# Layer 0's norm and projection in a four-layer float32 kernel: 1/std applied token-major behind two projections

## The chip, the cores and the metric

The kernel runs on one core of a Trainium2 chip. The metric is the device time of one execution, in microseconds (us). A core has five engines with queues of their own: PE (matrix products; loads of its stationary operand are shown as PEld), DVE (vector), ACT (scalar functions), POOL and SP. In this kernel SP issues nearly all transfers.

## The reference

Four layers run one after the other on x of 2 x 64 x 64 x 128 float32, that is 2 batches of 4096 tokens with 128 channels. Only the end of layer 0 matters here. Layer 0 scans 256 inner channels in four directions, and the sum of the four is y. Then it takes a layer norm over the 256 channels, gates with silu(z), projects back to 128 channels and adds to x:

```python
m = mean(y, channels); v = var(y, channels)
n = (y - m) / sqrt(v + 1e-5) * ln_w + ln_b      # per token, 256 channels
x = x + (n * silu(z)) @ W_out.T                  # 256 -> 128 channels
```

(These lines are a short form of the norm, the gate and the projection.) After it come layer 1 (a deformable convolution, which needs all of x), layer 2 (a scan with 256 states and a long convolution) and layer 3.

## The kernel before, in words

`layer0` loops over the two batches b. Each goes through three stages, and the pools of one stage are closed before the next opens:

1. The input: transposes of x (`to_channels`, L95), group norm, the products for z and for the inner channels, a 3 x 3 convolution. silu(z) is written to a DRAM buffer `zs` (L211). Stage 1 ends with the inner channels in `U`.
2. The scans (L349 to L406), under an order written out by hand. The result adds up in `Y`, a tile of 128 partitions by 2 halves by 4096 tokens: channels lie on partitions, half h holds channels 128h to 128h+127.
3. The norm and projection (L408 to L436), which the change rewrites. Here the Tile framework's planner orders the instructions on every engine from the program's order and its own costs; no order is written by hand.

Stage 3 loops over 8 pieces q of N = 512 tokens. For each piece:

- SP loads `zt`, the silu(z) of the piece, 512 KB (L414).
- PE forms the mean `pm`: a product of `mean_w`, a 128 x 128 matrix of 1/256, with Y. Its 512 columns all hold the mean, repeated on all 128 partitions (L417).
- DVE subtracts it from both halves of Y (L420), ACT squares into `sq` (L421), PE forms the variance `pq` in the same way as the mean (L424).
- `rsqrt` (L81 to L87) works on 128 x 512 elements, since every partition holds its copy: add eps, ACT's Sqrt, DVE's reciprocal, then one Newton step of four DVE instructions.
- DVE multiplies by ln_w and 1/std (L429), adds ln_b and multiplies by zt (L430), each for two halves.
- PE projects: for each of four blocks j of 128 tokens the stationary operand is Y's block and the moving one `w_out`, so that tokens come out on partitions (`po`, L434). DVE adds po to `Xb` (L436), which is x with tokens on partitions.

The pool `wk` has 2 buffers per tile, the PSUM pool `ps` has 6 buffers that all of pm, pq and po share.

Of the kernel before, what the change touches and what calls it, by code (L numbers as in the profile page):

```python
# [16 lines left out]
F32 = mybir.dt.float32  # L17
I32 = mybir.dt.int32
BF16 = mybir.dt.bfloat16
AF = mybir.ActivationFunctionType  # L20
ALU = mybir.AluOpType
# [4 lines left out]
P = 128  # L26
B, HH, WW, C = 2, 64, 64, 128
# [3 lines left out]
N = 512  # L31
# [45 lines left out]
def rsqrt(nc, pool, out, var, eps, shape, tag):  # L77

    v = pool.tile(shape, F32, name=f"{tag}_v", tag=f"{tag}_v")
    s = pool.tile(shape, F32, name=f"{tag}_s", tag=f"{tag}_s")  # L80
    nc.vector.tensor_scalar(v, var, eps, None, ALU.add)  # L81
    nc.scalar.activation(s, v, AF.Sqrt)
    nc.vector.reciprocal(out, s)
    nc.vector.tensor_tensor(s, out, out, ALU.mult)
    nc.vector.tensor_tensor(s, s, v, ALU.mult)
    nc.vector.tensor_scalar(s, s, -0.5, 1.5, ALU.mult, ALU.add)
    nc.vector.tensor_tensor(out, out, s, ALU.mult)  # L87
# [71 lines left out]
def layer0(k):  # L159
    tc, nc, ins, X = k.tc, k.nc, k.ins, k.X  # L160
    T = N
    NC = L // T
    with ExitStack() as es:
        enter = es.enter_context
        cst = enter(tc.tile_pool(name="l0c", bufs=1))
# [11 lines left out]
            nc.vector.tensor_copy(sel[a : a + 16], k.ident[a : a + 16, a : a + 16].unsqueeze(2).to_broadcast([16, 16, P]))  # L177
        w_out = cst.tile([P, 2, C], F32, name="w_out")
        nc.sync.dma_start(out=w_out, in_=ins["w_out0"].rearrange("(a p) c -> p a c", p=P))
        mean_w = cst.tile([P, P], F32, name="mean_w")  # L180
        nc.vector.memset(mean_w, 1.0 / 256)
        an = cst.tile([P, 8, 16], F32, name="an")
# [9 lines left out]
        for b in range(B):  # L192
            Xb = X[:, b * NTB : (b + 1) * NTB, :]
            with ExitStack() as e2:
                pre = e2.enter_context(tc.tile_pool(name=f"l0p{b}", bufs=1))
                wk = e2.enter_context(tc.tile_pool(name=f"l0w{b}", bufs=3))
                ps = e2.enter_context(tc.tile_pool(name=f"l0ps{b}", bufs=6, space=PSUM))
# [41 lines left out]
            Y = yb.enter_context(tc.tile_pool(name=f"l0y{b}", bufs=1)).tile([P, 2, L], F32, name="Y")  # L239

            with ExitStack() as e2:
                ch = e2.enter_context(tc.tile_pool(name=f"l0h{b}", bufs=2))
                sm = e2.enter_context(tc.tile_pool(name=f"l0s{b}", bufs=1))
                wk = e2.enter_context(tc.tile_pool(name=f"l0k{b}", bufs=3))
                bcp = e2.enter_context(tc.tile_pool(name=f"l0e{b}", bufs=2, space=DRAM))
                ps = e2.enter_context(tc.tile_pool(name=f"l0ys{b}", bufs=1, space=PSUM))
# [102 lines left out]
                with tc.manual_schedule():  # L349
                    rows, pcn, last, save = spread(ready[0][1], 0), c_row(ready[0][2], 0), None, None  # L350
                    for it, (kk, ci) in enumerate(todo):
                        c = at(it)[1]
                        uc, bc, cs, dt, du, ea = ready.pop()
                        f = T - 1 if kk >= 2 else 0
# [51 lines left out]
                    add_up(*last)  # L406

            with ExitStack() as e2:  # L408
                wk = e2.enter_context(tc.tile_pool(name=f"l0f{b}", bufs=2))
                ps = e2.enter_context(tc.tile_pool(name=f"l0fs{b}", bufs=6, space=PSUM))  # L410
                for q in range(8):
                    s = slice(q * N, (q + 1) * N)
                    zt = wk.tile([P, 2, N], F32, name="zt")
                    nc.sync.dma_start(out=zt, in_=zs[:, :, b * L + q * N : b * L + (q + 1) * N].rearrange("h p t -> p h t"))  # L414
                    pm = ps.tile([P, N], F32, name="pm", tag="ps")
                    for h in range(2):
                        nc.tensor.matmul(pm, mean_w, Y[:, h, s], start=h == 0, stop=h == 1)  # L417
                    sq = wk.tile([P, 2, N], F32, name="sq")
                    for h in range(2):
                        nc.vector.tensor_tensor(Y[:, h, s], Y[:, h, s], pm, ALU.subtract)  # L420
                        nc.scalar.activation(sq[:, h, :], Y[:, h, s], AF.Square)  # L421
                    pq = ps.tile([P, N], F32, name="pq", tag="ps")
                    for h in range(2):
                        nc.tensor.matmul(pq, mean_w, sq[:, h, :], start=h == 0, stop=h == 1)  # L424
                    rs = wk.tile([P, N], F32, name="rs")
                    rsqrt(nc, wk, rs, pq, 1e-5, [P, N], "yn")
                    for h in range(2):
                        o = Y[:, h, s]
                        nc.vector.scalar_tensor_tensor(o, o, k.v("ln_w")[:, h : h + 1], rs, ALU.mult, ALU.mult)  # L429
                        nc.vector.scalar_tensor_tensor(o, o, k.v("ln_b")[:, h : h + 1], zt[:, h, :], ALU.add, ALU.mult)  # L430
                    po = ps.tile([P, N], F32, name="po", tag="ps")
                    for j in range(4):
                        for h in range(2):
                            nc.tensor.matmul(po[:, j * P : (j + 1) * P], Y[:, h, q * N + j * P : q * N + (j + 1) * P], w_out[:, h, :], start=h == 0, stop=h == 1)  # L434
                    o = Xb[:, 4 * q : 4 * q + 4, :]
                    nc.vector.tensor_tensor(o, po.rearrange("p (a c) -> p a c", c=C), o, ALU.add)  # L436
            yb.close()


# [944 lines left out]
def kernel(tc, ins, out, stages=STAGES):  # L1384
    nc = tc.nc
    with ExitStack() as es:
# [8 lines left out]
        if two or "0" in stages or "1" in stages:  # L1395
            with tc.tile_pool(name="x01", bufs=1) as xp:
                k.X = xp.tile([P, NT, C], F32, name="X")
                move(nc, k.X, tokens(x))
                if "1" in stages:
                    table = [dr.tile([TS * TS, 4 * C], F32, name=f"table{b}") for b in range(B)]  # L1400
                    with tc.tile_pool(name="zt", bufs=1) as zp:
                        zero_table(k, zp, table)
                mix = None
                if two:
                    weights, mix = mixing_weights(k, dr)
                if "0" in stages:
                    layer0(k)
                if "1" in stages:
                    layer1(k, table, mix)
                elif two:  # L1410
                    with ExitStack() as e2:
                        mix(e2)
                if two:
                    norm_tokens(k, rs, sh)
                x = dr.tile([B * L, C], F32, name="x1")
                move(nc, tokens(x), k.X)
# [119 lines left out]
```

## Time and profile before

| | us |
|---|---|
| median of 3 runs (15821.19 to 15835.69) | 15821.78 |
| the profiled execution | 15825.24 |
| its span in the profile | 15823.2 |
| stage 3, batch 0: first L417 to the end of L436 | 2102.7 to 2254.6 |
| stage 3, batch 1: first L417 to the end of L436 | 4341.7 to 4493.7 |

The durations come from the one profiled execution. A line of the timeline has the start, the duration, the engine, the line of the kernel, the operation, output <- input with their sizes, and how many instructions are merged; in brackets stands how long the engine sat idle before it and what it waited for. A line of busy time by stretch has, after the stretch and its length, the busy time and number of instructions of PE, PEld, DVE, ACT and POOL, then the granted clock of PE as a share of full speed, the share of DMA time and GB/s.

### The profile page before, as it was taken

Reading aid. Unit: us, or ns where it says so; the run is one execution under the profiler, and the core shown is the slowest. Engines: PE = TensorE matmul, PEld = TensorE weight load, DVE = VectorE, ACT = ScalarE, POOL = GpSimd, SP = SyncE. Lnnn points to the kernel's source line nnn. Section 1 sums busy time; section 2 is a strip of 40 time slices with the busy share of each in tenths; the row PEclk is TensorE's granted clock in tenths of the full one; section 3 lists DMA queues with packets and bytes.
Section 4 is the critical chain, followed back from the end, with each engine's and each line's share of the span. In section 5 each row is a group of like instructions: output and inputs, shape, how many; then the busy total and the mean of one; then the engine's idle time right before and its main releaser. Section 6 shows DMA issues by size and latency. Waiting matters only on the chain.

```text
span 15823.2 us, 190331 instructions
## 1 busy us (share of the span) xinstructions
PE 11939.5 (75%) x69390; PEld 7104.0 (45%) x69390; DVE 13880.2 (88%) x12178; ACT 9839.5 (62%) x15907; POOL 13460.9 (85%) x5140
## 2 busy tenths in 40 slices
PE   6666666666667744567887879879788898898897
PEld 2222222222247721234554546546445555555565
DVE  7999978999954389999999999999999999999974
ACT  5656626666510057777777777777777777777752
POOL 6888828888738889999999999999999999999960
PEclk9999989999978866778998989989999999999998
DMA  2111111111146534455565556556666665665643
GB/s 79 70 70 70 70 44 67 70 70 70 64 143 185 161 133 148 168 172 187 196 193 179 187 179 198 197 185 202 193 190 198 190 204 196 191 203 195 191 163 129
DMA packets 1211433, 2373.40 MB, mean 150 GB/s; under 512 B 346744, under 2 KB 923896, under 8 KB 1044352
## 3 DMA queue, kind: packets, MB, share of 16 engines
q1 hardware_dynamic: 1163072, 2206.74, 42.3%
q0 software_dynamic: 46560, 153.18, 3.2%
q8 instruction: 548, 8.98, 0.2%
q14 instruction: 389, 3.19, 0.1%
q10 hardware_dynamic: 864, 1.32, 0.0%
HBM read 2018.49 MB, written 342.41 MB: 149 GB/s over the span
## 4 chain that ended last, share of the span: by engine, by line
POOL 35%; PE 12%; DVE 11%; DMA 3%; ACT 2%; issue 2%; SPq 0%; POOLq 0%; ACTq 0%; DVEq 0%
POOL S L1110 34%; DVE S L1166 10%; PE pef L994 6%; PE Z L1128 2%; DMA row<-drow 2%; PE acc L967 2%; PE pw L793 1%; POOL S L1116 1%; ACT ze L1134 1%; ACT dA L1164 1%; DMA w<-in_w_b_dram 0%; PE acc L1029 0%; ACT e L974 0%; DMA e<-mdr 0%; PE pt L95 0%
## 5 line engine op out<-in xcount | busy, mean ns | idle before, releaser
L1166 DVE TENSOR_TENSOR_SCAN S<-dA,S 128x512 f32<-128x512 f32 x8192 | 9225.0, 1201 | 385.8 <-ACT dA L1164 207.0
L1110 POOL TENSOR_TENSOR S<-row,g 128x4096 f32<-128x4096 f32 x1024 | 9101.7, 8894 | 266.0 <-DMA row<-drow 224.2
L1164 ACT ACTIVATE dA<-row,a_t 128x512 f32<-128x512 f32 x8192 | 5615.6, 692 | 2141.3 <-DVE S L1166 2108.3
L1128 PE MATMUL Z<-S,cv 128*32 128x256 f32 x32768 | 2506.0, 436 | 1481.7 <-ACT ze L1134 1215.6
L994 PE MATMUL pef<-hk,ur 128*128 128x256 f32 x14336 | 3510.4, 388 | 131.8 <-ACT e L974 120.5
L994 PEld LDWEIGHTS pef<-hk,ur 128*128 128x128 f32 x14336 | 2645.3, 191 | 1070.8 <-issue 562.8
L376 DVE TENSOR_TENSOR_SCAN S<-dA,S 128x1024 f32<-128x1024 f32 x1024 | 2339.1, 2284 | 242.4 <-ACT dA L374 96.1
L365 POOL TENSOR_TENSOR S<-du,br 128x1024 f32<-128x1024 f32 x1024 | 2408.6, 2355 | 137.8 <-DVE M L390 81.0
L1128 PEld LDWEIGHTS Z<-S,cv 128*32 128x32 f32 x32768 | 1002.5, 121 | 2691.5 <-issue 1291.9
L405 PE MATMUL yp<-M,ident 128*128 128x512 f32 x4096 | 2054.6, 626 | 2.9 <-DVE M L390 2.9
L405 PEld LDWEIGHTS yp<-M,ident 128*128 128x128 f32 x4096 | 817.6, 200 | 2092.5 <-issue 2054.1
L374 ACT ACTIVATE dA<-dt,an 128x511 f32<-128x511 f32 x2048 | 1406.9, 687 | 208.1 <-DVE S L376 131.0
L390 DVE TENSOR_TENSOR M<-S,pcn 128x1024 f32<-128x1024 f32 x1024 | 1250.4, 1221 | 106.9 <-DVE S L376 3.7
L334 PE MATMUL pcn<-cs,sel 80*128 80x512 bf16 x1024 | 406.2, 397 | 1188.4 <-DVE M L390 1177.8
L1134 ACT COPY ze<-Z 128x512 f32<-128x512 f32 x1024 | 1123.1, 1097 | 232.4 <-PE Z L1128 200.3
L967 PE MATMUL acc<-e,mw 128*128 128x512 f32 x1920 | 1043.1, 631 | 30.6 <-ACT e L974 29.9
L569 POOL DMA_INDIRECT G<-table,idx x576 | 805.5, 1399 | 203.1 <-issue 170.6
L994 PEld LDWEIGHTS pef<-hd,ur 128*128 128x128 f32 x4096 | 757.8, 194 | 491.1 <-issue 235.2
L994 PE MATMUL pef<-hd,ur 128*128 128x256 f32 (+1 forms) x4096 | 876.4, 340 | 101.5 <-ACT e L974 94.4
L378 ACT COPY stt<-S 128x2 f32<-128x2 f32 x896 | 168.9, 189 | 1082.1 <-DVE S L376 1079.0
L576 DVE TENSOR_TENSOR G<-G,wt 128x4608 f32<-128x4608 f32 x64 | 317.4, 4960 | 572.9 <-DMA G<-table,idx 499.6
L974 ACT COPY e<-pef 128x512 f32<-128x512 f32 x960 | 557.8, 587 | 109.9 <-PE pef L994 61.5
(327 smaller groups left out, 8052.3 us busy)
## 6 DMA issues: line engine op xcount, KB each, us to landing
row<-drow SPq DMA_DIRECT2D x1024, 1024.0 KB
br<-bc SPq DMA_DIRECT2D x256, 1024.0 KB
zd<-ze SPq DMA_DIRECT2D x1024, 256.0 KB
hk<-in_phi_dram SPq DMA_DIRECT2D x128, 576.5 KB
hk<-in_phi_dram SPq DMA_DIRECT2D x96, 704.5 KB
hd<-in_phi_dram SPq DMA_DIRECT2D x512, 128.5 KB
mw<-wdr SPq DMA_DIRECT2D x480, 128.0 KB
hk<-in_phi_dram SPq DMA_DIRECT2D x160, 320.5 KB
```

The source lines that it names most:

```text
L365: nc.gpsimd.tensor_tensor(S, du, br[:, n % 4, :].unsqueeze(1).to_broadcast([P, 2, T]), ALU.mult)
L374: nc.scalar.activation(dA[:, h, rest], dt[:, h, rest], AF.Exp, scale=an[:, kk * 2 + h, n : n + 1])
L376: nc.vector.tensor_tensor_scan(flat, dflat, flat, 0.0, ALU.mult, ALU.add)
L390: nc.vector.tensor_tensor(M, S, pcn.unsqueeze(1).to_broadcast([P, 2, T]), ALU.mult)
L405: nc.tensor.matmul(yp[:, h, :], k.ident, M[:, h, :], start=False, stop=n == 15)
L967: nc.tensor.matmul(acc.rearrange("p a s -> p (a s)"), ms[f][:, o, :], e, start=box["first"], stop="whole" in box and (f, o) == todo[-1])
L994: nc.tensor.matmul(pe[:, a, 256 - n :], ur[:, par, j, :], h[:, at : at + n], start=i == 0, stop=i + 1 == len(mm))
L1110: nc.gpsimd.tensor_tensor(S, row.unsqueeze(1).to_broadcast([P, 2, R, T]), g.unsqueeze(2).to_broadcast([P, 2, R, T]), ALU.mult)
L1128: nc.tensor.matmul(Z[32 * j : 32 * j + 32, q], cv[:, h, s], S[:, h, :, s], start=h == 0, stop=h == 1)
L1134: nc.scalar.copy(ze.rearrange("p q t e -> p q e t"), Z)
L1164: nc.scalar.activation(dA, row[:, j % R, :], AF.Exp, scale=a_t[:, h, d : d + 1])
L1166: nc.vector.tensor_tensor_scan(s, dA, s, 0.0, ALU.mult, ALU.add)
```

## The change

- Two weight tiles are made once, on POOL, ahead of the batches: `w_ow` is w_out with each row times ln_w, `w_ob` is w_out with each row times ln_b.
- The norm's scale is taken out of the projection. With c = y - m, `po` is the projection of c * zt through `w_ow` and `pb` that of zt through `w_ob`. The sum is x + pb + po / std. Tokens lie on partitions there, so 1/std is one number per partition and block.
- The variance comes out token-major too: `pv` has one column per block j, from 8 products whose stationary operand is a block of sq and whose moving operand is one column of mean_w. `rsqrt` works on 128 x 4 elements.
- DVE multiplies Y by zt in one instruction of 128 x 1024; ACT squares in one of 128 x 1024.
- The body is cut in two functions, and `projected(q - 1)` is called behind `centred(q)`. The pool `wk` has 3 buffers.

```diff
+        w_ow = cst.tile([P, 2, C], F32, name="w_ow")
+        w_ob = cst.tile([P, 2, C], F32, name="w_ob")
+        for h in range(2):
+            nc.gpsimd.tensor_scalar(w_ow[:, h, :], w_out[:, h, :], k.v("ln_w")[:, h : h + 1], None, ALU.mult)
+            nc.gpsimd.tensor_scalar(w_ob[:, h, :], w_out[:, h, :], k.v("ln_b")[:, h : h + 1], None, ALU.mult)
...
-                wk = e2.enter_context(tc.tile_pool(name=f"l0f{b}", bufs=2))
+                wk = e2.enter_context(tc.tile_pool(name=f"l0f{b}", bufs=3))
                 ps = e2.enter_context(tc.tile_pool(name=f"l0fs{b}", bufs=6, space=PSUM))
-                for q in range(8):
+
+                def centred(q):
+
                     s = slice(q * N, (q + 1) * N)
...
                     for h in range(2):
                         nc.vector.tensor_tensor(Y[:, h, s], Y[:, h, s], pm, ALU.subtract)
-                        nc.scalar.activation(sq[:, h, :], Y[:, h, s], AF.Square)
-                    pq = ps.tile([P, N], F32, name="pq", tag="ps")
-                    for h in range(2):
-                        nc.tensor.matmul(pq, mean_w, sq[:, h, :], start=h == 0, stop=h == 1)
-                    rs = wk.tile([P, N], F32, name="rs")
-                    rsqrt(nc, wk, rs, pq, 1e-5, [P, N], "yn")
-                    for h in range(2):
-                        o = Y[:, h, s]
-                        nc.vector.scalar_tensor_tensor(o, o, k.v("ln_w")[:, h : h + 1], rs, ALU.mult, ALU.mult)
-                        nc.vector.scalar_tensor_tensor(o, o, k.v("ln_b")[:, h : h + 1], zt[:, h, :], ALU.add, ALU.mult)
-                    po = ps.tile([P, N], F32, name="po", tag="ps")
+                    nc.scalar.activation(sq, Y[:, :, s], AF.Square)
+                    nc.vector.tensor_tensor(Y[:, :, s], Y[:, :, s], zt, ALU.mult)
+                    return zt, sq
+
+                def projected(q, zt, sq):
+                    pv = ps.tile([P, N], F32, name="pv", tag="ps")
                     for j in range(4):
                         for h in range(2):
-                            nc.tensor.matmul(po[:, j * P : (j + 1) * P], Y[:, h, q * N + j * P : q * N + (j + 1) * P], w_out[:, h, :], start=h == 0, stop=h == 1)
+                            nc.tensor.matmul(pv[:, j : j + 1], sq[:, h, j * P : (j + 1) * P], mean_w[:, 0:1], start=h == 0, stop=h == 1)
+                    rs = wk.tile([P, 4], F32, name="rs")
+                    rsqrt(nc, wk, rs, pv[:, :4], 1e-5, [P, 4], "yn")
+                    po = ps.tile([P, 4, C], F32, name="po", tag="ps")
+                    pb = ps.tile([P, 4, C], F32, name="pb", tag="ps")
+                    for o, src, w in ((pb, lambda h, j: zt[:, h, j * P : (j + 1) * P], w_ob), (po, lambda h, j: Y[:, h, q * N + j * P : q * N + (j + 1) * P], w_ow)):
+                        for j in range(4):
+                            for h in range(2):
+                                nc.tensor.matmul(o[:, j, :], src(h, j), w[:, h, :], start=h == 0, stop=h == 1)
                     o = Xb[:, 4 * q : 4 * q + 4, :]
-                    nc.vector.tensor_tensor(o, po.rearrange("p (a c) -> p a c", c=C), o, ALU.add)
+                    nc.vector.tensor_tensor(o, pb, o, ALU.add)
+                    for j in range(4):
+                        nc.vector.scalar_tensor_tensor(o[:, j, :], po[:, j, :], rs[:, j : j + 1], o[:, j, :], ALU.mult, ALU.add)
+
+                behind = None
+                for q in range(8):
+                    got = centred(q)
+                    if behind is not None:
+                        projected(q - 1, *behind)
+                    behind = got
+                projected(7, *behind)
```

## The prediction

> **What bounds the kernel now.** I read the page's slices first, then the busy time by stretch, then the timeline of one piece. The slices of DVE dip where each batch of layer 0 ends (slice 5 covers 1978 to 2373 us), and TensorE's granted clock dips there too:
>
> ```profile
> DVE  7999978999954389999999999999999999999974
> ...
> PEclk9999989999978866778998989989999999999998
> ```
>
> The two stretches from the last addition into Y to the last addition into X, by busy time of each engine:
>
> ```profile
> core 0: us, PE busy (x) PEld busy (x) DVE busy (x) ACT busy (x) POOL busy (x), PEclk, DMA share, GB/s
> 2101.32:2254.59 153.27, 62.28 (x192) 36.89 (x192) 92.50 (x106) 16.06 (x25) 0.56 (x1) 0.73 0.07 21
> 4340.30:4493.73 153.43, 62.46 (x192) 37.02 (x192) 92.50 (x106) 16.06 (x25) 0.51 (x4) 0.73 0.08 25
> ```
>
> No engine is full: of 153 us DVE works 92.5, PE 62, at a mean clock of 0.73. Nothing else runs there, so these 307 us are wholly exposed. The timeline of one piece says why:
>
> ```profile
> 2123.71 1.28 DVE L420 TENSOR_TENSOR Y<-Y,pm 128x512 f32<-128x512 f32 x2 [0.17 <-PE pm L417]
> 2124.43 1.23 ACT L421 ACTIVATE sq<-Y 128x512 f32<-128x512 f32 x2 [14.60 <-DVE Y L420]
> ...
> 2125.12 1.98 PE L424 MATMUL pq<-sq,mean_w 128*128 128x512 f32 x4 [1.44 <-ACT sq L421]
> ...
> 2127.14 0.69 DVE L81 TENSOR_SCALAR yn_v<-pq 128x512 f32<-128x512 f32 x1 [2.14 <-PE pq L424]
> ...
> 2128.53 3.35 DVE L83 RECIPROCAL rs<-yn_s 128x512 f32<-128x512 f32 x1 [0.69 <-ACT yn_s L82]
> ...
> 2134.55 1.42 DVE L429 SCALAR_TENSOR_TENSOR Y<-Y,pv,rs 128x512 f32<-128x512 f32 x2
> 2135.88 1.41 DVE L430 SCALAR_TENSOR_TENSOR Y<-Y,pv,zt 128x512 f32<-128x512 f32 x2
> 2136.68 0.50 PEld L434 LDWEIGHTS po<-w_out,Y 128*128 128x128 f32 x2 [10.41 <-DVE Y L430]
> ...
> 2142.21 0.69 DVE L436 TENSOR_TENSOR X<-po,X 128x512 f32<-128x512 f32 x1 [4.92 <-PE po L434]
> ```
>
> It is one chain through three engines. DVE waits 2.14 us for pq, 0.69 for the root, 4.92 for po; PE waits 10.41 us for DVE and then starts slow. From the first L420 (2104.93) to the eighth (2236.87) is 131.94 us, 18.85 a piece.
>
> [...] the granted clock is 0.50 from 2118 to 2120, right after that 10 us wait, and 1.00 from 2122. [...] the trace shows the second of two warm loads starting 0.11 us after the first (below). [...]
>
> **The change, part by part.** Prices of full-clock products of 128x128 and of products with one column:
>
> ```profile
> 15804.48 14.56 PE L1365 MATMUL py<-oe,G 128*128 128x128 f32 x128 [0.43 <-DVE oe L1359]
> ...
> 2264.85 0.30 PEld L136 LDWEIGHTS pm<-gn_mv,gmat 128*128 128x128 f32 x2 [4.89 <-issue]
> 2264.88 0.35 PE L136 MATMUL pm<-gn_mv,gmat 128*128 128x1 f32 x2 [4.68 <-issue]
> ```
>
> Each float32 product leaves two records. A 128x128 record costs 14.56/128 = 0.114 us at full clock, a 128x512 one 0.43 (16 of px in 7.03 us).
>
> *PE, per piece.* Kept: pm, 4 records, 1.72 us; po, 16 records, 16 x 0.114 = 1.83. Added: pb, 16 records, 1.83. Removed: pq, 4 records. Added for it: pv, 16 records with one column each. The trace has no run of such records. From below, a load at half the 0.11 spacing, 0.9 us; from above, no overlap at all, 16 x 0.19 (one load) = 3.0. I take 16 x 0.11 = 1.8. Sum 1.72 + 1.8 + 1.83 + 1.83 = **7.2 us**.
>
> *DVE, per piece.* Kept: two subtractions, 1.33 with the gap; one 128x512 addition, 0.72. Removed: six 128x512 steps of the inverse root, 0.69 + 3.35 + 0.69 + 0.69 + 0.43 + 0.69 = 6.5, and four 128x512 fused steps, 2.8. Added: six steps of 128x4, 0.195 from start to start as gn_s shows for 128x1, 1.2; one 128x1024 product, 1.25 (L390: 1.22); four fused 128x128 steps of PSUM. For those, 0.20 by the slope from 0.75 (512) and 0.40 (256, L855), 0.34 by L116's 128x128; I take 0.30, so 1.2. Sum **5.7 us**.
>
> *ACT, per piece.* One Square of 1024 (L305: 1.06) and a root of 0.20: 1.3 us, below both. No new table: before, Square and Sqrt alternate after one load.
>
> *Order.* The built order on PE is pv(q), pb(q), po(q), pm(q+2). pv(q+1) needs sq(q+1), whose mean came one turn (7.2 us) earlier; po needs Y x zt, which stands on DVE behind the addition of the previous pb, some 3 us before. So PE should wait for nobody. DVE waits for pb(q), then adds (0.72), multiplies (1.25), finishes the root (1.0), does the four steps (1.2), two subtractions (1.33), yn_v (0.2): 5.7 us, and pb(q+1) comes after 7.2. PE sets the pace with 1.5 us to spare. PSUM's six buffers: pm(q+2) takes the one that po(q-1) left, read by DVE a turn earlier. If that cover goes, the turn grows by what DVE is late.
>
> *DMA and queues.* SP issues the same eight zt of 512 KB per batch, with three buffers. Now zt(q+3) also waits for pb(q) on PE; behind it on SP stand only later zt, then gmat and w_in of the next batch, which wait for this stage's end as before. Two zt were on the way from 2096.24 to about 2101, 2.4 us each, against 14 us from release to use: free. If it slipped, each piece would wait 2.4 us at most.
>
> *POOL.* Four steps of 128x128 at the start, at L217's 0.585 us: 2.3 us. POOL stands idle after the frames (16.7 us) until the first scan's prologue, which comes after the convolutions, and these have reached only piece four by 65 us; w_out was asked for at 23.34. So nothing. Without that cover: 2.3 us once.
>
> *The sum.* First pm at 2102.7, two pm, the subtraction (2104.93 to 2106.2), Square to 2107.35: 4.65 us of start. Then 8 x (1.8 + 1.83 + 1.83) + 6 x 1.72 = 54.0, and the last four steps with their wait, 1.3: 60.0 us, where 2102.7 to 2254.59 was 151.9. Gain 92 per batch, **184** for both. Next late is PE itself. The to_channels that follows may start on a warm PE: 0 to 2 us a batch, taken as 0. The profiled execution took 15825.24 us (span 15823.2), 3.5 above the median 15821.78: 15825.24 - 184 = 15641, against the median **15638**.
>
> **The rivals.**
> *PE stays at half clock.* For it: 0.73 now[...]. Against: in the scan just before, with PE 59% busy and gaps of 1.43 us, the clock is 0.98. Price: pm 4 x 0.86, po and pb 16 x 0.222 each (3.66 us for the last piece's loads), pv 16 x 0.19: 13.6 a turn. Stage 4.65 + 8 x 10.2 + 6 x 3.4 + 1.3 = 108, gain 44 a batch: 15734.
> *DVE becomes the bound.* Its 14 steps wait on semaphores; 0.15 us more on each makes 7.8, with dear fused steps 8.4. Each turn loses up to 1.2, 10 us a batch: up to 15657. For it: a margin of only 1.5.
> *Every product taken alone, slower.* If PE could not overlap pairs and stayed cold, it would pay 0.56 for each one-column pair (L136 cold) and 0.80 for each 128x128 pair (first of L434): 4.5 + 6.4 + 6.4, pm 3.4, and DVE and ACT between po and the next pv exposed, 1.2 + 1.33 + 1.06 + 0.3: 24.6 a turn against 18.85, 92 us over both batches: 15914. It decides from 21 us a turn. Against: L1365 runs 128 records at 0.114.
> *The pieces do not overlap.* The planner could leave the chain whole: 7.2 of PE and about 5 of DVE and ACT between, 12 a turn; gain some 55 a batch, 15712. Against: the built order.
>
> **How the numbers follow.** 0.2% is 32 us, about what a measurement can tell from no change. Main case 0.78, with pv's bounds (-7, +10 a batch) and the warm start: 15620 to 15658. DVE bound 0.10, half clock 0.06, no overlap 0.03, products alone 0.02, something that eats the gain 0.01. The range goes to 15690 for mixes of DVE lateness and a PE that falls back to half clock now and then, and down to 15612: 0.88 or so inside by these cases. Faster 0.97, same 0.01, slower 0.02.
>
> **What would show it.** Right: each stage near 60 us, PE over 85% busy at clock 1.00, DVE's waits put down to pb and po, pv about 1.8 us a piece, reciprocal at 0.16. Wrong: clock 0.5 to 0.8 there; PE idle before po for DVE, or before pb for zt; pv above 3 us; a stage above 75 us.

## The result and the profile after

The changed kernel takes 15657.4 us, median of 4 runs (15643.86 to 15661.83), beside 15828.74 us (15821.19 to 15837.93) for the kernel before on the same chip: ratio 0.989, 95% interval 0.9873 to 0.9907. That is 171 us less, and it is clear of the 32 us. The profiled execution took 15656.0 us, with a span of 15653.8.

In the page's slices, counted from 0, PE's clock at the ends of the two batches went from 8 to 9 in slice 5 and from 7 to 8 in slice 11. DVE still dips in both (7 and 5), since slice 5 also holds the next batch's input stage, and slice 11 now holds only the last 8.6 us of the second stage and then the start of layer 1. So the step from 7 to 8 there is not the stage's own clock; the slices are too coarse for more:

```profile
DVE  7999978999853399999999999999999999999964
...
PEclk9999999999988867688987989989999999999998
```

The two stretches from the last addition into Y to the last into X, and five turns from the middle of the first, by busy time of each engine:

```profile
core 0: us, PE busy (x) PEld busy (x) DVE busy (x) ACT busy (x) POOL busy (x), PEclk, DMA share, GB/s
2104.85:2168.97 64.12, 60.61 (x416) 52.12 (x416) 42.25 (x114) 10.83 (x17) 0.00 (x0) 0.95 0.15 46
4252.38:4313.40 61.02, 57.36 (x416) 48.87 (x416) 42.32 (x115) 10.83 (x17) 0.00 (x0) 1.00 0.16 48
2121.54:2156.92 35.38, 35.38 (x261) 30.60 (x260) 24.03 (x65) 5.76 (x10) 0.00 (x0) 1.00 0.20 60
```

Each stretch was 153 us. PE is now full: in five turns it has no idle time, at clock 1.00, while DVE works 24.03 / 5 = 4.8 us of each 7.08. DVE fell from 92.5 to 42 us a batch. But the two batches differ by 3.1 us, and the first has a clock of 0.95. The timeline shows where:

```profile
2111.11 2.46 PE L437 MATMUL pv<-mean_w,sq 128*128 128x1 f32 x16 [0.96 <-ACT sq L429]
2113.42 3.76 PE L445 MATMUL pb<-w_ob,zt 128*128 128x128 f32 x16
2116.97 3.01 PE L445 MATMUL po<-w_ow,Y 128*128 128x128 f32 x16
...
2119.82 1.88 PE L425 MATMUL pm<-Y,mean_w 128*128 128x512 f32 x4
2121.54 1.84 PE L437 MATMUL pv<-mean_w,sq 128*128 128x1 f32 x16
2123.24 2.03 PE L445 MATMUL pb<-w_ob,zt 128*128 128x128 f32 x16
2125.11 1.95 PE L445 MATMUL po<-w_ow,Y 128*128 128x128 f32 x16
2125.31 0.69 DVE L447 TENSOR_TENSOR X<-pb,X 128x512 f32<-128x512 f32 x1 [1.73 <-PE pb L445]
2126.90 1.88 PE L425 MATMUL pm<-Y,mean_w 128*128 128x512 f32 x4
2128.12 1.13 DVE L449 SCALAR_TENSOR_TENSOR X<-po,rs,X 128x128 f32<-128x128 f32 x4
```

The lower seven lines are the forecast turn. From start to start pm takes 1.72 us, pv 1.70, pb 1.87, po 1.79: 7.08 in all. PE's lines have no bracket, so it waits for nobody; DVE's line has one, 1.73 us for pb. The first three lines are the first turn of the batch: the same products take up to twice as long, 8.7 us from pv's start to the next pm where the steady turn takes 5.4. A wait of 0.96 us for Square alone does not explain that.

### The profile page after: what moved, and what is told of

It reads as the page before. It is cut to its first block, busy times and chain, and to the rows that moved or that the text cites. A ratio compares the mean times of both kernels' runs of the same rounds, so it can differ in the third digit from the quotient of the medians.

```text
span 15653.8 us, 191264 instructions
## 1 busy us (share of the span) xinstructions
PE 11935.8 (76%) x69838; PEld 7130.0 (46%) x69838; DVE 13781.6 (88%) x12194; ACT 9829.6 (63%) x15891; POOL 13479.8 (86%) x5144
## 4 chain that ended last, share of the span: by engine, by line
POOL 34%; PE 13%; DVE 12%; DMA 3%; issue 2%; ACT 2%; SPq 0%; POOLq 0%; ACTq 0%; DVEq 0%
POOL S L1131 33%; DVE S L1187 11%; PE pef L1015 7%; PE Z L1149 2%; PE acc L988 2%; DMA row<-drow 1%; PE pw L814 1%; POOL S L1137 1%; ACT dA L1185 1%; ACT ze L1155 1%; DMA w<-in_w_b_dram 0%; PE acc L1050 0%; ACT e L995 0%; DMA e<-mdr 0%; PE pt L95 0%
## 5 line engine op out<-in xcount | busy, mean ns | idle before, releaser
L605 ACT COPY vt<-pv 128x512 f32<-128x512 f32 (+1 forms) x192 | 89.2, 480 | 863.2 <-remote 567.6
```

## The experiments

Throughout, "stage" is the time from the first pm to the end of the last fused step into X, batch 0 first and batch 1 after the stroke. In the kernel before it is 151.9 / 152.1 us, in the changed one 62.7 / 59.7. Line numbers shift by a few between kernels.

### The changed kernel and the kernel before once more

No edit in either.

> The changed kernel, unchanged, a second time. Two theories on the 12 us by which the profiled saving fell short of what the two stages gave (181 us by the start of layer 1, 169 at the end). (a) They are the scatter of the gather of layer 1 and of the scans of layer 2 from run to run: then the stages are again near 62 and 60 us, and the loss from layer 1's gather on comes out different, between -8 and +12 us, with a mean saving over the rounds of 170 to 185 us. (b) The changed kernel makes the later layers slower: then the loss is again 10 to 14 us, and the saving 166 to 172. Theory on the 3 us by which the first stage was longer than the second: PE fell to half clock in its first turn by chance of timing; then it may differ here, in either stage.

> The kernel before, unchanged, for a second profile. By theory (a), scatter, the gather of layer 1 (first to last indirect load) takes not 980.2 us again but something between 976 and 992; by (b), a slowing that the change brings, it takes 980 within 1.5 us. The two stages of norm and projection are 152 us each, within 1.

Measured: the changed kernel 15652.62 us (15642.72 to 15658.21), ratio 0.9884 (0.9867 to 0.9900) to 15834.27 for the kernel before in 23 runs. Stage 59.5 / 62.9. The slow first turn is now in batch 1 (its stretch has clock 0.95, that of batch 0 has 1.00), and costs 3.4 us (3.1 in the first profile). So it belongs to neither batch: it comes or stays away. The kernel before once more took 15825.98 us, stage 152.0 / 152.1.

### One piece behind alone, with the old arithmetic

```diff
-                for q in range(8):
+                def centred(q):
...
+                def projected(q, zt, sq):
...
+                behind = None
+                for q in range(8):
+                    got = centred(q)
+                    if behind is not None:
+                        projected(q - 1, *behind)
+                    behind = got
+                projected(7, *behind)
```

`centred` holds the load, the mean, the subtraction and Square, `projected` all from pq on, each as it was; `wk` has 3 buffers.

> The arithmetic of the kernel before, called one piece behind and with three buffers. If the overlap makes the gain, a stage comes near 65 us. If the cheap arithmetic makes it, this is far from that: DVE's 11.4 us of work a piece stay, and the built order keeps the wait for po in front of the next subtraction, so 11.4 + 4 = 15.5 us a turn, a stage of about 127 us, 15775 in all.

Measured: 15810.57 us, ratio 0.9985 (0.9978 to 0.9992); stage 137.9 / 137.9, that is 14.0 a batch. The timeline:

```profile
2134.41 0.80 PE L439 MATMUL po<-w_out,Y 128*128 128x128 f32 x2 [9.58 <-DVE Y L435]
...
2139.18 0.69 DVE L441 TENSOR_TENSOR X<-po,X 128x512 f32<-128x512 f32 x1 [4.17 <-PE po L439]
...
2151.40 0.76 PE L439 MATMUL po<-w_out,Y 128*128 128x128 f32 x2 [9.67 <-DVE Y L435]
```

A turn is 17.0 us (2134.41 to 2151.40). With the pieces overlapped by one, PE still waits 9.6 us for DVE's fused steps and DVE still 4.2 for po: the long chain of 128 x 512 steps is in every turn. I had expected 127, from 11.4 us of work and 4 of waiting for po; the sum lacked DVE's short waits for pq (0.43) and for the root (0.69), which stay.

### The new arithmetic alone, each piece projected in its own turn

```diff
-                behind = None
                 for q in range(8):
-                    got = centred(q)
-                    if behind is not None:
-                        projected(q - 1, *behind)
-                    behind = got
-                projected(7, *behind)
+                    projected(q, *centred(q))
```

> The changed arithmetic, with projected(q) called right after centred(q). If the arithmetic makes the gain: in the built order pm(q+1) stands behind po(q), so the chain po, pm, subtraction (1.33), Square (1.1), pv is bare once a turn: 7.1 + 2.5 = 9.6 us a turn, a stage of about 79 us, 36 us more than the changed kernel in all, 15693. If the overlap makes it, a turn is 14 us or more and a stage above 110 us. A third way: the gap of 2.5 us drops PE's clock, and a turn is 12 to 16 us.

Measured: 15749.44 us, ratio 0.9945 (0.9929 to 0.9962); stage 103.5 / 103.5. Busy time of the stage in batch 0, and the timeline of one turn:

```profile
core 0: us, PE busy (x) PEld busy (x) DVE busy (x) ACT busy (x) POOL busy (x), PEclk, DMA share, GB/s
2103.09:2206.59 103.50, 82.00 (x416) 71.05 (x416) 42.85 (x113) 11.37 (x17) 0.00 (x0) 0.77 0.09 26
```

```profile
2129.74 1.88 PE L425 MATMUL pm<-Y,mean_w 128*128 128x512 f32 x4
2134.09 1.95 PE L437 MATMUL pv<-mean_w,sq 128*128 128x1 f32 x16 [2.46 <-ACT sq L429]
2135.89 3.66 PE L445 MATMUL pb<-w_ob,zt 128*128 128x128 f32 x16
```

A turn is 12.7 us in the mean (11.4 to 13.6; the one shown is 11.4), so the third of the ways named above came true. Only 2.46 us of a turn are new idle time; the rest is products that take longer: pb 3.66 us here in place of 1.87, in other turns po too, up to 3.0. The clock of the stage is 0.77; in the turn shown it is 0.98 from 2134 to 2136 us and 0.50 from 2136 to 2138, where pb begins. So being one piece behind is worth 44 us a batch, and about half of that is not the wait but the clock that falls after it. The two halves of the change alone give 14.0 and 48.5 us a batch; together they give 89 to 92, more than the sum.

### The same, with pb ahead of pv

In the kernel above, the bias products need nothing from Square, so they can stand in the gap. They are taken out of their old place; the diff shows where they go.

```diff
                 def projected(q, zt, sq):
+                    pb = ps.tile([P, 4, C], F32, name="pb", tag="ps")
+                    for j in range(4):
+                        for h in range(2):
+                            nc.tensor.matmul(pb[:, j, :], zt[:, h, j * P : (j + 1) * P], w_ob[:, h, :], start=h == 0, stop=h == 1)
                     pv = ps.tile([P, N], F32, name="pv", tag="ps")
...
```

> The kernel e4_no_behind (each piece projected in its own turn) with one thing moved: the bias products pb are issued ahead of the variance's pv, where e4 has a gap on PE of 2.5 us in which pv waits for Square. Total PE work is the same. If e4 lost 24 of its 44 us a batch because that gap drops TensorE to half clock, the gap now shrinks to about 0.7 us (2.5 less pb's 1.85), the clock stays at 1.00, a turn is 7.1 + 0.7 to 0.9 = 7.8 to 8.0, the stage 65 to 70 us a batch and the whole about 15665 to 15680. If the 44 us come from the chain of dependences itself, whatever the clock, the stage stays at 95 us or more (15730 or above).

Measured: 15689.21 us, ratio 0.9911 (0.9894 to 0.9927); stage 74.1 / 76.9, 28 less a batch for a move within the turn. Busy time and timeline:

```profile
core 0: us, PE busy (x) PEld busy (x) DVE busy (x) ACT busy (x) POOL busy (x), PEclk, DMA share, GB/s
2102.76:2176.84 74.08, 66.85 (x416) 55.39 (x416) 43.45 (x113) 11.38 (x17) 0.00 (x0) 0.88 0.12 36
```

```profile
2133.46 1.95 PE L441 MATMUL pv<-mean_w,sq 128*128 128x1 f32 x16 [0.77 <-ACT sq L429]
2135.27 3.22 PE L447 MATMUL po<-w_ow,Y 128*128 128x128 f32 x16
...
2152.98 1.95 PE L441 MATMUL pv<-mean_w,sq 128*128 128x1 f32 x16 [0.76 <-ACT sq L429]
2154.79 2.03 PE L447 MATMUL po<-w_ow,Y 128*128 128x128 f32 x16
```

The gap shrank to 0.76 us as expected, and the chain theory (95 us or more) is out. But the stage is not 65 to 70: in five of the eight turns of batch 0 po still runs slow (3.22 in the upper pair), in three it does not (2.03 in the lower), after the same gap; in batch 1 it is six of eight. So the gap of 0.76 us alone does not tell the slow turns from the others. What stands between the gap and the slow po each time is pv, a run of one-column products.

### pv twice

```diff
-                    for j in range(4):
+                    for j in range(8):
                         for h in range(2):
-                            nc.tensor.matmul(pv[:, j : j + 1], sq[:, h, j * P : (j + 1) * P], mean_w[:, 0:1], start=h == 0, stop=h == 1)
+                            nc.tensor.matmul(pv[:, j : j + 1], sq[:, h, j % 4 * P : (j % 4 + 1) * P], mean_w[:, 0:1], start=h == 0, stop=h == 1)
```

> The changed kernel with the variance's one-column products issued twice in each piece, the second time into columns of pv that nothing reads: 16 more records a piece on PE, nothing more on DVE, ACT or DMA. This measures the one-column product and asks whether PE sets the pace. If PE does: 16 x 0.106 = 1.7 us more a turn, 8 turns, 13.6 a batch, the stage 73 to 74 us and the whole about 15684. If DVE sets the pace with PE waiting for it, the stage stays at 60 us. If the one-column products overlap with their neighbours more than their records show, the stage grows by less than 8.

Measured: 15713.84 us, ratio 0.9921 (0.9904 to 0.9938); stage 90.1 / 90.2. That is 30 us more, where the products themselves make 14.3 (8 x 1.79). Timeline, and busy time of the stage and of three slices of 2 us:

```profile
2135.08 3.63 PE L437 MATMUL pv<-mean_w,sq 128*128 128x1 f32 x32
2138.57 3.02 PE L445 MATMUL pb<-w_ob,zt 128*128 128x128 f32 x16
```

```profile
core 0: us, PE busy (x) PEld busy (x) DVE busy (x) ACT busy (x) POOL busy (x), PEclk, DMA share, GB/s
2105.86:2195.91 90.05, 87.93 (x544) 79.41 (x544) 41.38 (x113) 11.38 (x17) 0.00 (x0) 0.81 0.10 30
...
2128.00:2130.00 2.00, 2.00 (x15) 2.00 (x16) 0.16 (x1) 0.20 (x1) 0.00 (x0) 0.79 0.00 0
2130.00:2132.00 2.00, 2.00 (x12) 2.00 (x11) 1.09 (x2) 0.00 (x0) 0.00 (x0) 0.50 0.04 8
2132.00:2134.00 2.00, 2.00 (x13) 1.75 (x13) 1.76 (x8) 0.00 (x0) 0.00 (x0) 0.86 0.83 252
```

The pv run takes 3.49 us from start to start where it took 1.70, 0.109 a record: the price of a one-column product holds. PE is busy 2.00 of 2.00 us in each slice and has no gap, and yet its clock falls to 0.50 at the end of the run or behind it, in each of the eight turns of both batches. The fall shown, worked out from the three slices, lasts (1 - 0.79) / 0.5 x 2 + 2 + (1 - 0.86) / 0.5 x 2 = 3.4 us.

### pv twice, cut in two

Against the changed kernel, the second half of the products goes behind pb:

```diff
                                 nc.tensor.matmul(o[:, j, :], src(h, j), w[:, h, :], start=h == 0, stop=h == 1)
+                        if o is pb:
+                            for j in range(4):
+                                for h in range(2):
+                                    nc.tensor.matmul(pv[:, 4 + j : 5 + j], sq[:, h, j * P : (j + 1) * P], mean_w[:, 0:1], start=h == 0, stop=h == 1)
```

> The same 16 extra one-column records a piece as e6_pv_twice, but issued after the bias products pb, so that the run of one-column products is cut in two of 1.7 us with 1.9 us of 128x128 products between. In e6 the granted clock fell to 0.50 right after each unbroken run of 3.4 us, with PE 100% busy. Theory: TensorE's clock counts an unbroken stretch of one-column products, and a gap with it, as idle. Then the clock stays at 1.00 here, a turn is 7.1 + 1.7 = 8.8 us, the stage 73 to 75 us and the whole about 15685. Rival: what counts is the share of one-column products in the whole turn (3.4 of 8.8 us). Then the clock falls as in e6 and the stage stays near 90 us.

Measured: 15679.54 us, ratio 0.9906 (0.9889 to 0.9922); stage 75.4 / 75.4. The same instructions as in the run before, in another order, and 14.7 us less a batch:

```profile
core 0: us, PE busy (x) PEld busy (x) DVE busy (x) ACT busy (x) POOL busy (x), PEclk, DMA share, GB/s
2100.16:2175.57 75.41, 73.28 (x544) 64.76 (x544) 41.59 (x113) 10.72 (x17) 0.00 (x0) 0.98 0.12 36
```

The clock is 0.98, so the rival (the share of one-column products in a whole turn) is out: what differs between 0.81 and 0.98 is only where the one-column products lie. One sum then fits all these stages: 59.5 us (the stage at clock 1.00), plus added work or gaps, plus half of the time at half clock, which is (1 - clock) / 0.5 of the stage (there a product takes twice as long: the 16 of pb 3.76 us in the slow first turn, 2.03 or less in the steady ones). With the clock taken as measured, it shows where the time went, not why the clock fell.

| kernel | gap + pv, us | added, us | half the cold time, us | sum | stage, batch 0 |
|---|---|---|---|---|---|
| changed, slow first turn | 0.96 + 1.7, once | 0 | 62.7 x 0.05 = 3.1 | 62.6 | 62.7 |
| own turn, pb first | 0.76 + 1.8 | 8 x 0.76 = 6.1 | 74.1 x 0.12 = 8.9 | 74.5 | 74.1 |
| pv twice | 0 + 3.5 | 8 x 1.79 = 14.3 | 90.1 x 0.19 = 17.1 | 90.9 | 90.1 |
| pv twice, cut in two | 0 + 1.7, twice | 8 x 1.71 = 13.7 | 75.4 x 0.02 = 1.5 | 74.7 | 75.4 |
| own turn | 2.46 + 1.8 | 8 x 2.46 = 19.7 | 103.5 x 0.23 = 23.8 | 103.0 | 103.5 |

A stretch of 1.7 us never brought the clock down in the middle of a stage of the changed kernel, one of 2.5 to 2.7 did in 13 of 20 turns (all of pb first and the first turns of the changed kernel), and one of 3.5 or more did in all 32. But an unbroken stretch, as the theory had it, is not needed. Late in the stage of the kernel cut in two the clock falls once in each batch, with no gap on PE and with full products between two runs of 1.7 us (the stage's clock is 0.98, and pb takes 3.65 us):

```profile
2162.56 1.84 PE L449 MATMUL pv<-mean_w,sq 128*128 128x1 f32 x16
2164.26 1.36 PE L445 MATMUL po<-w_ow,Y 128*128 128x128 f32 x10
2165.46 1.85 PE L437 MATMUL pv<-mean_w,sq 128*128 128x1 f32 x16
2167.17 3.65 PE L445 MATMUL pb<-w_ob,zt 128*128 128x128 f32 x16
```

The clock's own records in the first two profiles, of the kernel before and of the changed one, say more. In each of the two, the falls to half clock start whole multiples of 3.41 us apart, within 0.03 us, as on a grid, and in the stages they last 6.83 us (changed) or 10.24 and 13.65 (before), two, three and four times that. Lay PE's products on this grid, call every product but the one-column ones full, and count each from its start to the next one's, or to its end where PE then waits. The first turns of the changed kernel's two batches, in such windows:

```profile
core 0: us, PE busy (x) PEld busy (x) DVE busy (x) ACT busy (x) POOL busy (x), PEclk, DMA share, GB/s
2108.94:2112.35 3.41, 2.45 (x14) 1.44 (x13) 2.98 (x5) 1.91 (x2) 0.00 (x0) 1.00 0.00 0
2112.35:2115.76 3.41, 3.41 (x18) 3.41 (x18) 1.56 (x3) 1.70 (x3) 0.00 (x0) 0.50 0.00 0
2115.76:2119.18 3.42, 3.42 (x18) 3.42 (x18) 1.43 (x6) 0.00 (x0) 0.00 (x0) 0.50 0.27 59
2119.18:2122.59 3.41, 3.41 (x22) 2.45 (x21) 1.98 (x6) 0.00 (x0) 0.00 (x0) 1.00 0.25 94
4255.92:4259.34 3.42, 2.46 (x12) 1.15 (x10) 2.94 (x5) 1.39 (x2) 0.00 (x0) 1.00 0.00 0
4259.34:4262.75 3.41, 3.41 (x32) 3.41 (x33) 2.33 (x4) 2.21 (x3) 0.00 (x0) 1.00 0.00 0
```

The first line holds the wait of 0.96 us, 1.24 us of pv and 1.21 of full products, and the next two have clock 0.50; the fifth holds the same wait, 0.72 us of pv and 1.73 of full products, and the next stays at 1.00. In the kernel cut in two, the 3.41 us up to the slow pb, from 2163.76 to 2167.17, hold 1.20 us of po, with the end of one pv run and all of the next. Over both stages of the two traces, the 17 windows at full clock with at most 1.21 us of full products were followed by half clock, and the 64 with at least 1.68 us by full clock. At half clock, where a product takes twice as long, the 35 windows with at most 2.63 us were followed by half clock and the 15 with at least 2.87 by full clock. In this count waits and one-column products are both left out; only one of the 17, the one shown, holds one-column products, and no run was made to test the count. A turn of pv twice, 10.49 us, is close to three times 3.41, so if its clock falls on such a grid too, its turns lie nearly alike on it and are not eight separate tests.

### Two, four and six more products on DVE

```diff
                     nc.vector.tensor_tensor(Y[:, :, s], Y[:, :, s], zt, ALU.mult)
+                    for _ in range(2):
+                        pad = wk.tile([P, N], F32, name="pad")
+                        nc.vector.tensor_tensor(pad, zt[:, 0, :], zt[:, 1, :], ALU.mult)
```

The other two have `range(4)` and `range(6)`.

> The changed kernel with two more DVE products of 128x512 in each piece (zt x zt into a tile that nothing reads), 2 x 0.71 = 1.4 us, inside the 1.73 us that DVE waits for pb in each turn. If PE sets the pace, the stage stays at 60 us, within 1.5, and DVE's wait for pb falls to about 0.3 us a turn. If DVE is the bound or its work delays what PE needs (the subtractions, Y x zt), the stage grows by up to 8 x 1.4 = 11 us.

> As e7, with four such products in each piece: 4 x 0.71 = 2.8 us, more than the 1.73 us that DVE has to spare. If PE sets the pace until DVE fills the turn, a turn is now DVE's own 5.3 + 2.8 = 8.1 us against 7.1, the stage 66 to 69 us; DVE has no wait for pb left and PE waits for DVE's Y. If the spare time is larger than the waits show, the stage stays at 60; if DVE's work were in PE's chain already, it grows by 8 x 2.8 = 22.

> As e7 and e8, with six extra DVE products of 128x512 a piece. In e8 a turn stayed at 7.08 us with DVE full (4.8 of its own and four of 0.60 to 0.68). Two more should show in full: a turn of 4.8 + 6 x 0.61 = 8.4 us, the stage 60 + 8 x 1.3 = 70 to 73 us a batch. If DVE still had room, the stage stays at 60 to 64.

Measured, one run of each: 15665.94, 15666.1 and 15674.23 us; stages 60.9 / 65.1, 64.1 / 62.0 and 65.4 / 67.5, with a slow first turn in the second batch of the first kernel and in the first batch of the second. Beside a like batch of the changed kernel, two products cost 1.4 and 2.2 us: near what was expected, and at the stage's ends, not in its turns. Four cost hardly more (1.4 and 2.4), which I had not expected (66 to 69). Busy time of three turns with four:

```profile
core 0: us, PE busy (x) PEld busy (x) DVE busy (x) ACT busy (x) POOL busy (x), PEclk, DMA share, GB/s
2125.00:2146.20 21.20, 21.20 (x158) 18.33 (x158) 20.14 (x56) 3.79 (x6) 0.00 (x0) 1.00 0.24 76
```

PE stays full, and DVE is busy for 95% of the time. So DVE had more to spare than the 1.73 us of its wait for pb: its other waits are spare too, and independent steps of 128 x 512 start 0.60 us apart, not 0.72. With six, the timeline:

```profile
2126.16 1.88 PE L425 MATMUL pm<-Y,mean_w 128*128 128x512 f32 x4
2126.85 2.48 DVE L433 TENSOR_TENSOR pad<-zt 128x512 f32<-128x512 f32 x4
...
2133.24 1.88 PE L425 MATMUL pm<-Y,mean_w 128*128 128x512 f32 x4
...
2134.85 2.48 DVE L433 TENSOR_TENSOR pad<-zt 128x512 f32<-128x512 f32 x4
```

DVE's turn is now 8.00 us and PE's still 7.08: DVE falls behind by 0.9 us a turn. PE feels it only in the last turns, where it waits 0.43 us for DVE and then 1.04 for Square. Behind this second wait stands pv, and behind pv the products run slow (in batch 1 pb takes 3.76 us and po 3.08). The clock of the stage in batch 0 is 0.95, that is about 6.5 us at half clock (0.05 / 0.5 x 65.4), or 3.3 us of the 5.9 by which the stage grows (65.4 - 59.5). I had put 8.4 on DVE's turn and 70 to 73 on the stage: each extra product was priced too dear, and the first turns run on DVE's reserve. So the bound passes to DVE between four and six extra products, but the stage is too short to show a full turn of DVE's length on PE.

### Without the bias product

```diff
-                    for o, src, w in ((pb, lambda h, j: zt[:, h, j * P : (j + 1) * P], w_ob), (po, lambda h, j: Y[:, h, q * N + j * P : q * N + (j + 1) * P], w_ow)):
+                    for o, src, w in ((po, lambda h, j: Y[:, h, q * N + j * P : q * N + (j + 1) * P], w_ow),):
...
-                    nc.vector.tensor_tensor(o, pb, o, ALU.add)
```

> The changed kernel without the bias product pb and its addition into X (so this part of the result is left out): 16 records of 128x128 fewer a piece on PE, one 128x512 addition fewer on DVE. If PE sets the pace, a turn falls by pb's own 1.87 us to 5.2, the stage to 44 to 47 us a batch. If DVE's chain or the pv to rs to po order sets it, it falls by less than 0.7 a turn (the addition), the stage stays above 54. One-column products are then 1.7 of 5.2 us; if their share matters to the clock, it falls below 1.00 and the stage is 50 or more.

Measured: 15615.79 us, one run; stage 45.7 / 49.1, the second with a slow first turn. One turn, from pm to pm:

```profile
2127.95 1.88 PE L425 MATMUL pm<-Y,mean_w 128*128 128x512 f32 x4
...
2133.24 1.88 PE L425 MATMUL pm<-Y,mean_w 128*128 128x512 f32 x4
```

5.29 us, less by 1.79, nearly the whole 1.87 of pb: PE's products set the pace.

### The squares and the bias path in bf16

The squares and their column of 1/256, and zt and w_ob of the bias path, are rounded to bf16; the rest stays float32.

```diff
-        w_ob = cst.tile([P, 2, C], F32, name="w_ob")
+        w_ob = cst.tile([P, 2, C], BF16, name="w_ob")
+        mean_h = cst.tile([P, 2], BF16, name="mean_h")
...
-                    sq = wk.tile([P, 2, N], F32, name="sq")
+                    sq = wk.tile([P, 2, N], BF16, name="sq")
...
+                    zh = wk.tile([P, 2, N], BF16, name="zh")
+                    nc.scalar.copy(zh, zt)
```

zh takes zt's place in pb, mean_h that of mean_w in pv.

> A version that should be faster: the squares, zt for the bias path, and the weights of both are bf16, so that pv and pb leave 8 records each a piece, not 16; ACT gets one more 128x1024 copy (1.06 us, to 2.3 of its turn). If PE still sets the pace: pv 0.85, pb 0.9, po 1.79, pm 1.72, a turn of 5.3 us, the stage 44 to 47 us a batch, 13 to 16 less than the changed kernel, the whole about 15625. If DVE's 4.8 us and its waits set the pace in its place: 5.6 to 6 a turn, the stage 48 to 52, about 15635.

Measured: 15622.36 us (15614.1 to 15634.06), ratio 0.9867 (0.9850 to 0.9883); stage 42.4 / 42.2. It lies 213 us under its kernel before (15835.74), the changed kernel 182 under its own (15834.27), and the ranges of the two do not touch. Timeline and busy time of some turns:

```profile
2127.11 1.88 PE L427 MATMUL pm<-Y,mean_w 128*128 128x512 f32 x4
2128.82 0.34 PE L441 MATMUL pv<-mean_h,sq 128*128 128x1 bf16 x8
2129.03 0.61 PE L449 MATMUL pb<-w_ob,zh 128*128 128x128 bf16 x8
2129.80 2.02 PE L449 MATMUL po<-w_ow,Y 128*128 128x128 f32 x16 [0.17 <-DVE rs L83]
```

```profile
core 0: us, PE busy (x) PEld busy (x) DVE busy (x) ACT busy (x) POOL busy (x), PEclk, DMA share, GB/s
2125.00:2146.20 21.20, 18.80 (x157) 14.85 (x156) 20.95 (x73) 7.87 (x12) 0.00 (x0) 0.95 0.17 50
```

From start to start pv takes 0.21 us for 8 records, 0.026 each, where I had kept the float32 price of 0.106. The bound has moved: DVE is busy 20.95 of 21.20 us, po waits for DVE, and a turn is 4.56 us. This is the fastest version measured that leaves nothing out.

## Why the prediction was right, step by step

**The level.** Forecast 15638, measured 15657.4, inside 15612 to 15690. Of the 19 us, 7 are the kernel before itself, whose median was 15828.74 in this comparison and 15821.78 in the forecast; the other 12 to 13 are a gain of 171 in place of 184. The repeat gave 182.

**The stage.** Forecast 60.0 us; measured 59.5 with the clock at 1.00 throughout, 62.7 to 62.9 with a slow first turn. In both profiles one batch was of each kind, so the two stages together gain 181.5 us of the 184. The forecast had "may start on a warm PE" for what follows the stage, but nothing in its sum for the stage's own first turn, and a fall to half clock only as a reason for the range's upper end; that missing term is 3.1 to 3.4 us.

**PE's terms.** pm 1.72 against 1.72, pv 1.70 against 1.8, pb 1.87 and po 1.79 against 1.83 each: 7.08 against 7.2. The row that was missing, one-column products, fell near the middle of its bounds of 0.9 and 3.0; such a record takes 0.106 us, and the loads of its blocks start 0.11 us apart.

**DVE's terms.** Forecast 5.7 us with 1.5 to spare; measured 4.8 busy with 2.3 to spare. Four fused steps take 1.13 us against 1.2, so 0.30 each was near; the rest was too dear because the forecast spaced every step as if it waited for the one before. Four extra products a turn without a longer turn show the reserve.

**Order and queues.** PE has no wait in the steady turns (busy 35.38 of 35.38 us), so neither zt's load nor the buffers of PSUM hold it up. POOL's four steps ran from 27.9 to 33.4 us, 5.4 us where 2.3 were priced, but beside the input stage, so nothing waited. to_channels' 32 products took 3.68 us in place of 5.55, and the first pz came 1.4 us sooner behind the stage (14.6 in place of 16.0): inside the 0 to 2 that was left at nothing.

**The rivals.** Half clock was turned down by the scan's gaps of 1.43 us at a clock of 0.98. That comparison was too weak: it has gaps but no one-column products behind them. The doubled pv shows that the danger was real. That the change stays clear of it was not derived, and was in part luck: its other windows of 3.41 us hold at least 1.71 us of full products, where the one before the fall in its slow first turn held 1.21. "The pieces do not overlap" was priced at 12 us a turn for 5 us of idle time; the kernel that does just that has 12.7, but from 2.46 us of idle time and some 3 of lost clock. The number was near, its reason was not. DVE as the bound and products taken alone did not occur.

**What stays open.** At the start of layer 1 the changed kernel's profile is 181.8 us ahead; at the end it is 15823.2 - 15653.8 = 169.4 ahead. In the repeats the lead falls from 186.2 to 170.4. Of the loss, 8.3 us lie in layer 1's gather, whose code is untouched: 980.2 us before and 988.5 after, 980.6 and 986.6 in the repeats. By what was expected of the repeats, the gather of the kernel before speaks for a slowing that the change brings, the mean saving of 182 for scatter. On the chip of the repeats the two experiments of the order alone and of the arithmetic alone have 987.2 and 986.3; on two other chips the experiments' kernels have 979.7 to 985.0. So whether the change slows the gather is open. The cause was not found.

## What to carry to other kernels

When one engine has become the bound, take its turn apart by start-to-start times of its own products, and test it by adding a little to each engine: here the bias product taken from PE shortened the turn by nearly its own length, and 2.4 us more of DVE in each turn did not lengthen it. Moving work by one iteration was worth 44 us a batch here, about twice the wait that it removed (8 x 2.46 = 19.7 us): with the wait the granted clock of the stage was 0.77, without it 0.95 to 1.00. In judging that, look at one-column products together with the waits: in one run of 3.5 us a turn they left the stage at clock 0.81 with no wait in its steady turns, and with the bias products put between two runs of 1.7 us, at 0.98.

## What was not expected of the hardware

- A run of 3.5 us of one-column float32 products, with PE shown busy all the time, brought the granted clock to 0.50 for 3.4 us (worked out from slices of 2 us); the same products in two runs of 1.7 us left the stage at 0.98, with one such fall a batch.
- In the changed kernel's profile the same wait of 0.96 us ahead of pv was followed by 6.83 us at half clock in batch 0 and by full clock in batch 1. Of the window of 3.41 us around that wait, products with more than one column took 1.21 us in the first case and 1.73 in the second.
- A one-column record took 0.106 us in float32 and 0.026 in bf16, a factor of 4 for a record; pv left 16 records a piece in float32 and 8 in bf16.
- Independent DVE steps of 128 x 512 start 0.60 us apart (the extra products), dependent ones 0.72 (the inverse root of the kernel before).
